# Weight and bias of a normalisation: one GpSimd operation over four chunks in place of one for each chunk

## The chip, the cores and the metric

The kernel runs on one core of a Trainium2 chip. The metric is device time in microseconds of one launch. The median of three runs is 2514.97 us (2506.65 to 2515.73). The engines are named as in the profile: PE is TensorE, DVE is VectorE, ACT is ScalarE, POOL is GpSimd, SP is SyncE, which here only issues DMAs.

## The reference

Four cross-attention layers run over `x` of 2 x 1024 tokens with 288 channels, with a context of 2 x 154 tokens. Layers 0 and 1 are blocks of three parts with quantised linear maps; layers 2 and 3 are plain attention over two parts of the context. A block of layers 0 and 1, cut to what matters:

```python
def quant_act(x):
    s = max(abs(x), axis=-1) / 127 + 1e-8
    q = clip(round(x / s), -127, 127)
    return q, s, sum(q, axis=-1)

def layer_norm(x, g, b, eps):
    return (x - mean(x)) * rsqrt(var(x) + eps) * g + b      # over the 288 channels

h = layer_norm(x, ln1_g, ln1_b, 1e-6);  q8, s, sm = quant_act(h)
q, k, v = (quant_linear(q8, s, sm, w, b) for w, b in (wq1.., wk1.., wv1..))
x = x + quant_linear(*quant_act(attn(q, k, v)), wo1, bo1)   # self-attention, 16 heads of 18
h = layer_norm(x, ln2_g, ln2_b, 1e-5)                       # then attention over the context
...
h = layer_norm(x, ln3_g, ln3_b, 1e-5)                       # then 288 -> 1152, gelu, 1152 -> 288
```

The weight `g` and the bias `b` of each normalisation are rows of 288 numbers, the same for every token.

## The kernel before

The tokens lie on the 128 partitions in 16 chunks of 128 tokens (`x` is `[128, 16, 288]`, float32, and stays in SBUF). Work on tokens is done in groups of four chunks (`HC = 4`, 512 tokens).

`ln_quantise` normalises and quantises one such group. VectorE computes mean and variance of each chunk (`bn_stats`, `bn_aggr`, L406 and L407) and adds epsilon (L408); GpSimd raises to the power -1/2 (L411); VectorE makes the shift (L413). Then, chunk by chunk, ScalarE writes `x * rstd + shift` into the tile `h` of `[128, 4, 288]` (L419), and engine `eng` multiplies by the weight and adds the bias, in place (L427): two operations of 128x288 for each of four chunks. `eng` is GpSimd, but for the first two calls, which `prepare_first` makes with VectorE. The weight and the bias are broadcast to all partitions beforehand, in a tile `ln` of `[128, 2, 288]` (`load_ln`, L175).

`quantise` follows: VectorE takes the largest magnitude of each chunk's rows in one reduction over the whole tile (L370), a scale (L371) and its reciprocal (L372); GpSimd writes the reciprocal into extra columns in three bfloat16 parts (L377 to L380); VectorE scales each chunk (L382), ScalarE rounds it and sums it (L386), VectorE writes the sums (L396, L397). Then TensorE transposes (L443), and the linear maps run.

`ln_quantise` runs 24 times: for the self-attention of each layer and batch (tile names `ah` for the two on VectorE, `alh` for six), for the attention over the context (`blh`, eight), and for the feed-forward part (`clh`, eight).

All this is side work. The main stream is attention: TensorE makes logits twice, once by query for their row maxima, which VectorE reduces (L597, L604), and once by key (L656), which ScalarE exponentiates (L658) and TensorE multiplies with the values (L670). GpSimd splits the maxima in three parts (L210 to L213), TensorE transposes them (L572), and ScalarE's and SP's DMAs bring them back as extra rows of the queries. GpSimd also splits queries and keys (L507, L514), adds results to `x` (L469), fills constant rows (L106), finishes weight preparation (L245 to L260; VectorE's share is L222 to L240), and issues the DMAs that load weights (L197, L1393).

What order the instructions have: the program interleaves the main stream with the side work by counts (`beside` and the generators' `yield`s), and the whole body stands in one block that a planner orders, `tc.block(schedule_with_timeline_sim=True)`: it places each instruction on its engine by a clock of its own. Each engine then runs its own list strictly in that order. The order on GpSimd in the trace isn't that of the program: other operations stand between the eight of a normalisation at several places.

Of the kernel before, what the change touches and what calls it, by code (L numbers as in the profile page):

```python
# [13 lines left out]
ALU = mybir.AluOpType  # L14
AX = mybir.AxisListType

P = 128
B, S, C, T = 2, 1024, 288, 154
# [3 lines left out]
HC = 4  # L22
# [31 lines left out]
def tile_xattn(ctx: ExitStack, tc: tile.TileContext, ins: dict, out: bass.AP):  # L54
# [81 lines left out]
    def big(name):  # L136
        return work.tile([P, FF], F32, tag="big", name=name, bufs=3)

    def bf(name):
        return work.tile([P, 3 * HQ], BF16, tag="bf", name=name, bufs=3)  # L140
# [11 lines left out]
    def view(ap, **kw):  # L152
        names = list(kw)
        return ap.rearrange(f"p ({' '.join(names)}) -> p {' '.join(names)}", **kw)
# [209 lines left out]
    def quantise(h, q, s, n, width, name):  # L364

        st = small.tile([P, 4, HC], F32, tag="qstat", name=name)
        am, rs, qs, r = (st[:, j, 0:n] for j in range(4))
        nc.vector.tensor_reduce(am, h, AX.X, ALU.max, apply_absolute_value=True)  # L370
        nc.vector.tensor_scalar(s, am, 1.0 / 127.0, 1e-8, ALU.mult, ALU.add)  # L371
        nc.vector.reciprocal(rs, s)  # L372

        def cols(k0, k1):
            return q[:, :, width + k0 : width + k1]

        nc.gpsimd.tensor_copy(cols(9, 12), rs.unsqueeze(2).to_broadcast([P, n, 3]))  # L377
        nc.gpsimd.tensor_tensor(r, rs, q[:, :, width + 9], ALU.subtract)
        nc.gpsimd.tensor_copy(cols(7, 9), r.unsqueeze(2).to_broadcast([P, n, 2]))
        nc.gpsimd.tensor_tensor(q[:, :, width + 6], r, q[:, :, width + 7], ALU.subtract)  # L380
        for c in range(n):
            nc.vector.tensor_scalar(  # L382
                h[:, c, :], h[:, c, :], rs[:, c : c + 1], MAGIC, ALU.mult, ALU.add
            )
        for c in range(n):
            nc.scalar.activation(  # L386
                q[:, c, 0:width],
                h[:, c, :],
                AF.Identity,
                bias=nmagic,  # L390
                scale=1.0,
                accum_out=qs[:, c : c + 1],
            )
        sums = qs.unsqueeze(2).to_broadcast([P, n, 3])
        hi = q[:, :, width : width + 6 : 2]
        nc.vector.tensor_scalar(hi, sums, -1.0, None, ALU.mult)  # L396
        nc.vector.scalar_tensor_tensor(  # L397
            q[:, :, width + 1 : width + 6 : 2], sums, -1.0, hi, ALU.mult, ALU.subtract
        )

    def ln_quantise(c0, ln, eps, s, name, h=None, q=None, eng=nc.gpsimd):
        st = small.tile([P, HC, 6], F32, tag="bn", name=f"{name}st")
        mv = small.tile([P, HC, 2], F32, tag="mv", name=f"{name}mv")
        rstd = small.tile([P, HC], F32, tag="rstd", name=f"{name}r")
        for c in range(HC):
            nc.vector.bn_stats(st[:, c, :], x[:, c0 + c, :])  # L406
            nc.vector.bn_aggr(mv[:, c, :], st[:, c, :])  # L407
        nc.vector.tensor_scalar(  # L408
            rstd, mv[:, :, 1:2].rearrange("p c a -> p (c a)"), eps, None, ALU.add
        )  # L410
        nc.gpsimd.tensor_tensor(rstd, rstd, neghalf, ALU.pow)  # L411
        shift = small.tile([P, HC], F32, tag="shift", name=f"{name}sh")
        nc.vector.scalar_tensor_tensor(  # L413
            shift.unsqueeze(2), mv[:, :, 0:1], -1.0, rstd.unsqueeze(2), ALU.mult, ALU.mult
        )
        if h is None:
            h = view(big(f"{name}h"), c=HC, w=C)
        for c in range(HC):
            nc.scalar.activation(  # L419
                h[:, c, :],  # L420
                x[:, c0 + c, :],
                AF.Identity,
                bias=shift[:, c : c + 1],
                scale=rstd[:, c : c + 1],
            )
            for j, op in ((0, ALU.mult), (1, ALU.add)):
                eng.tensor_tensor(h[:, c, :], h[:, c, :], ln[:, j, :], op)  # L427
        if q is None:
            q = bf(f"{name}q")
        q = view(q[:, 0 : HC * CZ], c=HC, w=CZ)  # L430
        quantise(h, q, s, HC, C, f"{name}qs")
        return q
# [517 lines left out]
    class SelfAttention:  # L950
# [26 lines left out]
        def prepare(self):  # L977
            w, b, name = self.w, self.b, self.name
            self.begin()
            for hf in range(2):  # L980
                c0 = b * 8 + hf * HC
                s = small.tile([P, HC], F32, tag="st", name=f"{name}st")
                q = ln_quantise(c0, w["ln"], 1e-6, s, f"{name}l")
                yield 8
                qT = transposed(q, f"{name}t")
                sb = token_scales(s, f"{name}sb")
                yield 2
                yield from weights_of(2, linear_T(qT, w["k"], sb, self.k[hf], f"{name}k"))
                self.values(hf, qT, s)
                yield 3  # L990
                yield from weights_of(2, linear_T(qT, w["q"], sb, self.q[hf], f"{name}q"))

        def prepare_first(self):
# [12 lines left out]
            def normalise(hf):  # L1006
                h = apool.tile([P, HC, C], F32, tag="a", name=f"{name}h", bufs=2)
                s = small.tile([P, HC], F32, tag="st", name=f"{name}st")
                c0 = b * 8 + hf * HC
                q = ln_quantise(  # L1010
                    c0, w["ln"], 1e-6, s, f"{name}l", h, tile(), nc.vector
                )
                scales.append(s)
                qs.append(q)
# [151 lines left out]
    def cross_attention(w, b, name):  # L1166
# [71 lines left out]
        def queries(hf):  # L1238
            s = small.tile([P, HC], F32, tag="st", name=f"{name}st")
            q = ln_quantise(b * 8 + hf * HC, w["ln"], 1e-5, s, f"{name}l")  # L1240
            yield 8
            qT = transposed(q, f"{name}t")
            sb = token_scales(s, f"{name}sb")
            rows.append(new_rows(f"{name}qr"))
            yield 2
            yield from weights_of(2, linear_T(qT, w["q"], sb, rows[hf], f"{name}q"))
# [491 lines left out]
```

## Time and profile before

| | us |
|---|---|
| median of three runs | 2514.97 |
| the profiled execution | 2516.42 |
| its span, first to last instruction | 2514.6 |
| PE busy | 1970.1 (78%) |
| DVE busy | 1865.4 (74%) |
| ACT busy | 1394.9 (55%) |
| POOL busy | 786.6 (31%) |
| L427 on POOL, 176 instructions of 128x288 | 135.1 (49.4 + 49.1 + 36.6) |
| L427 on DVE, 16 instructions of 128x288 | 6.2 |
| L419 on ACT, one chunk | 0.61 |
| mean granted TensorE clock | 0.867 |

A line of a group reads: source line, engine, operation, output<-inputs, shapes, count, busy us and mean ns of one, idle time of the engine before them and what ended it. A line of the timeline reads: start and length in us of neighbouring instructions of one kind taken together, engine, line, operation, tiles, count, and in brackets the idle time before and what ended it. The chain is the work that ended last, followed back step by step; its pieces read start, length, what.

### The profile page before, as it was taken

What the parts mean: (1) busy time and instruction counts of PE and PEld (TensorE: products, weight loads), DVE (VectorE), ACT (ScalarE), POOL (GpSimd) and SP (SyncE); (2) the same over time, 40 slices, a digit from 0 to 9 for tenths busy, and PEclk for the clock granted to TensorE, in tenths of its full rate; (3) what the DMA queues carried; (4) which work ended last, traced back from release to release, by engine and by line L of the source; (5) the groups of instructions that cost most, each with busy time, mean ns of one, the idle gap of its engine ahead of it and who ended that gap; (6) DMA issues with size and microseconds to landing.
All of it is one profiled execution on the core that took longest, in us unless ns stands there. A gap on an engine that the chain in (4) does not pass through costs nothing.

```text
span 2514.6 us, 33307 instructions
## 1 busy us (share of the span) xinstructions
PE 1970.1 (78%) x10524; PEld 851.0 (34%) x10524; DVE 1865.4 (74%) x4465; ACT 1394.9 (55%) x2639; POOL 786.6 (31%) x1794
## 2 busy tenths in 40 slices
PE   1679998888776878887678678887777887788987
PEld 1233333332333233323333233333334333443443
DVE  6789997899775659998569849994346786555665
ACT  3267766555576665556666355557654444654443
POOL 5424224211325451132353530223255132422210
PEclk9589998899787989999889689896888888888998
DMA  3423212211001322110032131100133210212221
GB/s 95 150 66 94 70 42 55 75 55 28 16 9 44 113 74 58 44 29 13 7 101 72 29 88 49 34 9 12 32 82 92 73 47 27 64 45 80 75 65 36
DMA packets 160129, 141.56 MB, mean 56 GB/s; under 512 B 44251, under 2 KB 156467, under 8 KB 159888
## 3 DMA queue, kind: packets, MB, share of 16 engines
q1 hardware_dynamic: 148528, 120.58, 16.6%
q0 software_dynamic: 3840, 13.37, 2.1%
q10 hardware_dynamic: 7584, 5.47, 1.2%
q8 instruction: 84, 1.38, 0.2%
q14 instruction: 93, 0.76, 0.1%
HBM read 96.60 MB, written 39.37 MB: 54 GB/s over the span
## 4 chain that ended last, share of the span: by engine, by line
PE 25%; DVE 15%; ACT 10%; DMA 6%; issue 3%; POOL 3%; SPq 1%; ACTq 0%; DVEq 0%; POOLq 0%
DVE L_xattn_amxh L604 4%; PE L_xattn_aato L670 4%; PE L_xattn_o L1484 3%; PE L_xattn_aats L656 3%; ACT L_xattn_aatse L658 3%; PE L_xattn_ato L670 2%; PE L_xattn_ats L656 2%; PE L_xattn_amx L597 2%; PE L_xattn_q L453 2%; DVE L_xattn_batse L742 2%; ACT L_xattn_atse L658 1%; DMA L_xattn_bqT<-L_xattn_bmxsr 1%; DVE L_xattn_bmxm L637 1%; DVE L_xattn_bmxn L642 1%; DVE L_xattn_mxn L642 1%
## 5 line engine op out<-in xcount | busy, mean ns | idle before, releaser
L658 ACT ACTIVATE L_xattn_aatse<-L_xattn_aats 128x512 f32<-128x512 f32 x1024 | 574.6, 595 | 300.5 <-PE L_xattn_aats L656 283.4
L604 DVE TENSOR_REDUCE L_xattn_amxh<-L_xattn_amx 128x1 f32<-128x512 f32 x1024 | 658.7, 677 | 54.6 <-PE L_xattn_amx L597 50.6
L656 PE MATMUL L_xattn_aats<-L_xattn_aqT,kT 120*128 120x512 bf16 x1024 | 392.9, 409 | 99.9 <-ACT L_xattn_aatse L658 61.6
L597 PE MATMUL L_xattn_amx<-kT,L_xattn_aqT 108*128 108x512 bf16 x1024 | 394.7, 418 | 64.2 <-DVE L_xattn_amxh L604 46.7
L670 PE MATMUL L_xattn_aato<-L_xattn_aatse,L_xattn_av 128*32 128x512 f32 x2048 | 296.9, 649 | 28.7 <-ACT L_xattn_aatse L658 26.3
L656 PEld LDWEIGHTS <-kT 120*128 120x128 bf16 x1024 | 96.2, 101 | 334.3 <-issue 297.6
L658 ACT ACTIVATE L_xattn_atse<-L_xattn_ats 86x512 f32<-86x512 f32 (+1 forms) x256 | 142.5, 589 | 109.6 <-PE L_xattn_ats L656 102.2
L597 PEld LDWEIGHTS <-L_xattn_aqT 108*128 108x128 bf16 x1024 | 103.4, 103 | 218.0 <-issue 164.9
L642 DVE TENSOR_REDUCE L_xattn_mxn<-L_xattn_mx 128x2 f32<-128x172 f32 (+1 forms) x512 | 125.1, 302 | 35.1 <-PE L_xattn_mx L627 34.6
L743 ACT ACTIVATE L_xattn_batse<-L_xattn_batse 128x512 f32<-128x512 f32 x160 | 100.0, 626 | 85.6 <-DVE L_xattn_batse L742 82.5
L656 PE MATMUL L_xattn_ats<-L_xattn_qT,L_xattn_kT 120*86 120x512 bf16 (+1 forms) x256 | 101.5, 432 | 40.6 <-DMA L_xattn_qT<-L_xattn_mxsr 20.0
L742 DVE TENSOR_TENSOR L_xattn_batse<-L_xattn_bats,L_xattn_bmT 128x512 f32<-128x512 f32 x160 | 107.3, 680 | 23.9 <-PE L_xattn_bats L670 12.2
L637 DVE TENSOR_TENSOR L_xattn_bmxm<-L_xattn_bmx,L_xattn_bm 128x308 f32<-128x308 f32 x256 | 114.8, 464 | 5.5 <-PE L_xattn_bmx L627 4.6
L642 DVE TENSOR_REDUCE L_xattn_bmxn<-L_xattn_bmxm 128x2 f32<-128x308 f32 x256 | 113.8, 457 | 0.3
L1484 PE MATMUL L_xattn_o<-wo,L_xattn_p 128*128 128x288 f32 x320 | 100.8, 452 | 6.2 <-DVE L_xattn_p L815 4.7
L670 PEld LDWEIGHTS L_xattn_aato<-L_xattn_aatse,L_xattn_av 128*32 128x32 f32 x2048 | 42.0, 111 | 162.1 <-ACT L_xattn_aatse L658 131.9
L627 PE MATMUL L_xattn_bmx<-L_xattn_bkT,L_xattn_bqT 108*128 108x154 bf16 x512 | 76.5, 248 | 16.7 <-DVE L_xattn_amxh L604 8.2
L627 PE MATMUL L_xattn_mx<-L_xattn_kT,L_xattn_qT 108*128 108x154 bf16 x512 | 72.0, 257 | 22.1 <-DVE L_xattn_mxn L642 7.6
L843 DVE STREAM_TRANSPOSE L_xattn_atT<-L_xattn_ato 128x512 f32<-128x512 f32 x64 | 45.7, 713 | 57.4 <-PE L_xattn_ato L670 47.0
L1351 PE MATMUL L_xattn_co<-L_xattn_wfc2t,L_xattn_cgT 117*128 117x288 bf16 x320 | 63.6, 350 | 22.4 <-ACT L_xattn_cgT L1348 21.5
L670 PE MATMUL L_xattn_ato<-L_xattn_atse,L_xattn_v 68*32 68x512 f32 (+1 forms) x512 | 74.1, 651 | 5.2 <-ACT L_xattn_atse L658 4.7
L1484 PEld LDWEIGHTS L_xattn_o<-wo,L_xattn_p 128*128 128x128 f32 x320 | 64.0, 210 | 30.7 <-DVE L_xattn_p L815 6.0
(629 smaller groups left out, 3729.2 us busy)
## 6 DMA issues: line engine op xcount, KB each, us to landing
kT<-L_xattn_akr SPq DMA_DIRECT2D x192, 72.0 KB
L_xattn_aqT<-L_xattn_aqr SPq DMA_DIRECT2D x192, 72.0 KB
L_xattn_bqT<-L_xattn_bqr SPq DMA_DIRECT2D x192, 72.0 KB
L_xattn_qT<-L_xattn_r SPq DMA_DIRECT2D x192, 72.0 KB
L_xattn_akr<-L_xattn_akst SPq DMA_DIRECT2D x16, 324.0 KB
L_xattn_aqr<-L_xattn_aqst SPq DMA_DIRECT2D x16, 324.0 KB
L_xattn_bqr<-L_xattn_bqst SPq DMA_DIRECT2D x16, 324.0 KB
L_xattn_r<-L_xattn_qst SPq DMA_DIRECT2D x16, 324.0 KB
```

The costliest lines, as they stand in the source:

```text
L597: nc.tensor.matmul(sp, lhsT=qt[:KR, j, c * P : (c + 1) * P], rhs=kt[:KR, j, a * 512 : (a + 1) * 512], start=True, stop=True,)
L604: nc.vector.tensor_reduce(halves[:, a, c, j, :], sp, AX.X, ALU.max, negate=True)
L627: nc.tensor.matmul(sp[:, j * T : (j + 1) * T], lhsT=qt[:KR, 2 * a + j, c * P : (c + 1) * P], rhs=kt[:KR, 4 * g + 2 * a + j, 0:T], start=Tr ...
L637: nc.vector.tensor_tensor(lm, of, mask[:, c : c + 1, 0:T].to_broadcast([P, 2, T]), ALU.add)
L642: nc.vector.tensor_reduce(nm[:, c, 2 * a : 2 * a + 2, n], of[:, :, k0:k1], AX.X, ALU.max, negate=True,)
L656: nc.tensor.matmul(sp, lhsT=keys(j), rhs=qt[:KM, j, :], start=True, stop=True)
L658: nc.scalar.activation(e, sp, AF.Exp)
L670: made = nc.tensor.matmul(po[32 * i : 32 * i + 32, :], lhsT=lhsT, rhs=rhs, start=start, stop=stop)
L742: nc.vector.tensor_tensor(e, sp, maskT[:, m, :], ALU.add)
L743: nc.scalar.activation(e, e, AF.Exp)
L1351: nc.tensor.matmul(ps, lhsT=gT[:, k, :], rhs=qw2[:, k, :], start=(k == 0), stop=(k == 9),)
L1484: nc.tensor.matmul(ps, lhsT=t[:, c * P : (c + 1) * P], rhs=wo[:, u0 + u, :], start=(u == 0), stop=(u == len(tiles) - 1),)
```

## The change

The two operations leave the loop over the chunks. They run once each, over all four chunks, with the weight's and the bias's row read four times over:

```diff
@@ ln_quantise @@
         for c in range(HC):
             nc.scalar.activation(h[:, c, :], x[:, c0 + c, :], ...)
-            for j, op in ((0, ALU.mult), (1, ALU.add)):
-                eng.tensor_tensor(h[:, c, :], h[:, c, :], ln[:, j, :], op)
+        for j, op in ((0, ALU.mult), (1, ALU.add)):
+            eng.tensor_tensor(
+                h, h, ln[:, j : j + 1, :].to_broadcast([P, HC, C]), op
+            )
         if q is None:
             q = bf(f"{name}q")
```

Each element has the same arithmetic in the same order. Of 192 operations of 128x288, 176 on GpSimd and 16 on VectorE, 48 of 128x1152 are left, 44 and 4. The multiplication now reads what all four ScalarE instructions have written. Nothing else of the program's text differs; lines below it move by two.

## The prediction

> **What bounds the kernel now.** I read the page first, then the groups of GpSimd by shape, the line of the change (L427) with its waits, the timeline at each of its places, and the chain.
>
> ```profile
> PE 1970.1 (78%) x10524; PEld 851.0 (34%) x10524; DVE 1865.4 (74%) x4465; ACT 1394.9 (55%) x2639; POOL 786.6 (31%) x1794
> PE 25%; DVE 15%; ACT 10%; DMA 6%; issue 3%; POOL 3%; SPq 1%; ACTq 0%; DVEq 0%; POOLq 0%
> ```
>
> TensorE and VectorE set the time; GpSimd is busy for 31% and has 3% (some 75 us) of the chain that ended last. So what GpSimd saves counts only where it stands on that chain, or where another engine waits for it.
>
> ```profile
> L427 POOL TENSOR_TENSOR L_xattn_blh<-L_xattn_blh,L_xattn_ln 128x288 f32<-128x288 f32 x64 | 49.4, 798 | 9.9 <-ACT L_xattn_blh L419 9.6
> L427 POOL TENSOR_TENSOR L_xattn_clh<-L_xattn_clh,L_xattn_ln 128x288 f32<-128x288 f32 x64 | 49.1, 795 | 14.9 <-ACT L_xattn_clh L419 14.8
> L427 POOL TENSOR_TENSOR L_xattn_alh<-L_xattn_alh,L_xattn_ln 128x288 f32<-128x288 f32 x48 | 36.6, 798 | 6.0 <-ACT L_xattn_alh L419 6.0
> L507 POOL TENSOR_TENSOR L_xattn_bqy<-L_xattn_bqy,L_xattn_bqst 108x512 f32<-108x512 f32 x24 | 27.8, 1164 | 42.8 <-ACT L_xattn_bqst L506 37.4 <-DMA L_xattn_bqT<-L_xattn_bqr 5.4
> L212 POOL TENSOR_TENSOR L_xattn_amxn<-L_xattn_amxn,L_xattn_amxst 128x16 f32<-128x16 f32 x32 | 7.2, 224 | 1.8
> ```
>
> The changed work is 64 + 64 + 48 = 176 GpSimd instructions, 22 normalisations of eight, plus 16 on VectorE in the first two. Who waits for them, from the view of that line:
>
> ```profile
> its engine sat idle before it (us, times) until:
>   ACT L_xattn_clh L419: 14.8, 4
> ...
> who waited for it (us, times):
>   PEld L443: 0.9, 1
> ```
>
> Nobody, to speak of. VectorE's reduction L370, the first reader of the normalised chunks, never stands idle for GpSimd. One ordinary place in the timeline shows why:
>
> ```profile
> 386.59 2.17 ACT L419 ACTIVATE L_xattn_blh<-x,L_xattn_blsh,L_xattn_blr 128x288 f32<-128x288 f32 x4
> 387.28 6.08 POOL L427 TENSOR_TENSOR L_xattn_blh<-L_xattn_blh,L_xattn_ln 128x288 f32<-128x288 f32 x8 [2.40 <-ACT L_xattn_blh L419]
> 388.23 3.08 DVE L604 TENSOR_REDUCE L_xattn_amxh<-L_xattn_amx 128x1 f32<-128x512 f32 x5 [0.36 <-PE L_xattn_amx L597]
> 395.94 1.34 DVE L370 TENSOR_REDUCE L_xattn_blqs<-L_xattn_blh 128x4 f32<-128x1152 f32 x1
> ```
>
> ScalarE writes the four chunks back to back, GpSimd follows 0.69 us after the first, ends at 393.36, and L370 starts 2.58 us later from VectorE's own queue. Over all 22 places this margin is 1.1 to 44 us, mostly 2.6 to 6.4.
>
> **The change, step by step.**
>
> *One instruction of 128x1152.* No row shows it. Fixed part from the 16-element row: about 200 ns; the rest of 796 ns by four: 200 + 4 x 596 = 2.58 us. Low end: the 108x512 row adds 368 ns for 224 elements, so 796 + 864 x 1.64 = 2.21 us. High end: no fixed cost saved, 4 x 0.796 = 3.18 us. I take 2.58: same engine, partitions and type.
>
> *GpSimd time.* Eight back to back start 0.76 us apart (6.08 / 8); two take some 5.1 us (range 4.4 to 6.3). Saving 22 x 1.0 = 22 us of its queue, nearly all beside TensorE and VectorE. On the chain the timeline of pieces has 24 of the 176, 17.6 us together, at three places only (1714, 1828, 2145); the largest pieces:
>
> ```profile
> 1713.82 3.81 POOL L_xattn_clh L427 x5
> 2145.53 4.50 POOL L_xattn_clh L427 x6
> ```
>
> Times 1.0/6.08 this is **-2.9 us**.
>
> *A wait added.* The first instruction now needs ScalarE's fourth chunk: the series starts 2.2 us after the first ACTIVATE, not 0.69. In 11 of the 22 places GpSimd starts later than that first chunk anyway (behind its own queue, or with the last chunk); there nothing or little is lost. In the other 11 it loses 1.5 us and wins 1.0 back: +0.5, against margins of 1.1 and more in front of L370, so nothing; without that cover 11 x 0.5 = 5.5 us. Behind the waiting instruction stand GpSimd's small splits of the maxima (L210 to L213) and the third parts (L514), whose readers are TensorE's transposes and SP's transfers. On the chain the wait costs: at 1714 1.45 us (start 1713.82, last chunk 1715.28), at 1828 0.9, at 2145 0.4: **+2.7 us**.
>
> *The start of the kernel*, on VectorE:
>
> ```profile
> 35.01 2.18 ACT L419 ACTIVATE L_xattn_ah<-x,L_xattn_alsh,L_xattn_alr 128x288 f32<-128x288 f32 x4 [13.99 <-DVE L_xattn_alsh L413]
> 35.97 3.03 DVE L427 TENSOR_TENSOR L_xattn_ah<-L_xattn_ah,L_xattn_ln 128x288 f32<-128x288 f32 x8
> 36.14 3.64 POOL L245 TENSOR_SCALAR L_xattn_wq1sq<-L_xattn_wq1w 108x864 bf16<-108x864 f32 x1 [2.75 <-DVE L_xattn_wq1w L240]
> ```
>
> VectorE's rows (444 ns at 288, 0.68 us at 512 in L507) give 1.05 ns an element: 444 + 864 x 1.05 = 1.35 us, two 2.65. They begin at 37.2 and end near 39.9, not at 38.99: +0.9. On the other side L245, 0.90 us just before this, took 3.64 beside the eight; with VectorE waiting until 37.2 it could finish, and the queue behind it leads to TensorE's first transposes at 49.00: down to -2.7. I take **0**, between them: later in that queue L377 waits for VectorE's row maximum anyway.
>
> *Longer holds of a shared port.* Today:
>
> ```profile
> 1269.48 1.93 DVE L228 SCALAR_TENSOR_TENSOR L_xattn_wfc_0s<-L_xattn_wfc_0s 96x3 f32<-96x3 f32 x1
> ...
> 1269.49 1.16 POOL L507 TENSOR_TENSOR L_xattn_aky<-L_xattn_aky,L_xattn_akst 108x512 f32<-108x512 f32 x1
> 1270.61 0.79 POOL L427 TENSOR_TENSOR L_xattn_alh<-L_xattn_alh,L_xattn_ln 128x288 f32<-128x288 f32 x1
> ```
>
> A VectorE instruction with two SBUF inputs, 0.15 us elsewhere, stood 1.93 us, until two GpSimd instructions had ended; L604, which reads PSUM, isn't touched (five in 3.08 us at 388.23). Summing over the trace each VectorE duration above the tenth percentile of its line and shape (those over 0.15 us), 52 us are lost so, 23 of them beside L427, and 9.9 of the 52 (19%) lie on the chain. Here a rule speaks against the change: the Trainium skill, "SBUF — State Buffer", in the table of terms and the summary of ports, says that the pair shared by VectorE and GpSimd is held for the full instruction and that the loser fully blocks. By the row alone (so much wait per us of GpSimd work) 23 us shrink with the work, 23 x 5.1/6.08: -3.7 us, -0.7 on the chain, and the whole sum would come to -0.9. By the rule the wait grows with the instruction: 8.4 of the 23 us are four waits that already spanned several instructions and stay; the other 14.5 us are some 24 waits of 0.6 us, which become half an instruction, 1.29 us, at 5.1/6.08 as many occasions: 26 us, so +11.5, of which 19% counts: **+2.2 us**. I take the rule, since the row shows such a wait ending with the GpSimd instruction.
>
> *Order.* The order on each engine comes from a planner that runs its own clock, so new durations can swap neighbours anywhere. No row prices that: one 0.6 us instruction on the wrong side at each of 22 places, all of one sign, is 13 us either way. I take 0 and keep 13 for the range.
>
> Sum: -2.9 + 2.7 + 0 + 2.2 = **+2.0 us** on this execution's 2516.42 us (span 2514.6, 1.8 around it). The execution lies 1.5 us above the median of the runs, 2514.97; on that the forecast is **2517 us**.
>
> **Rivals.**
>
> *Slower: the port decides.* The place is weight preparation (L224 to L240), the quantisations (L382, L396, L397) and the context's keys (L510), with L604 queued behind and TensorE waiting for L604. For it: from 126 to 504 us VectorE is busy 331 of 378 us, so waits there have no slack. If each of the 24 waits lasts a whole instruction less what it is now, half the way (1.0 us more each, 24 us), and 74% (VectorE's busy share) counts, it is +18: 2533 us. From 17 us of added waits at that share it passes 0.5% (12.6 us), about what a measurement of this kernel can tell from no change. Against it: only 19% counts in the chain today.
>
> *Faster: the shorter series is passed on.* In the 11 places where the series began late it would end 0.9 us sooner; -9.9 if L370 moves up with it, -2.7 at the start, -2.9 on the chain: about 2500 us. Against it: L370's margins.
>
> *The two cost what eight did.* If reading the same row four times breaks the instruction up, 3.18 us each: 6.36, +0.8 on the chain's 17.6 us in place of -2.9, +2.7 for the wait, +2.2 or a little more for the port: 2521 us, still no change.
>
> *The new order alone* moves either of these by its 13 us.
>
> **How the numbers follow.** Nearly even 0.46, port 0.28, passed on 0.21, no cheaper 0.05. Likeliest: 2517, its own range 2504 to 2530 (the order's 13 us). For 8 in 10 both other cases are reached with part of their spread: 2496 to 2541. Beyond 0.5% means under 2502.4 or over 2527.5: faster 0.25 (most of "passed on", an edge of the first), slower 0.30, same 0.45.
>
> **What would show it.** The changed line with 44 GpSimd instructions at 2.2 to 2.7 us and 4 at 1.35 on VectorE; GpSimd's busy time near 760 us; the series starting with ScalarE's last chunk; L370 still not waiting for GpSimd. Right on the port: VectorE durations of L228, L382 or L510 reaching 2 us beside L427, and VectorE's busy time up by about 10 us. Wrong if L370 waits for L427, if the splits L210 move late and TensorE waits for their transposes, or if groups far from L427 change their idle time by more than 10 us: then the order decided.

## The result and the profile after

The changed kernel took 2526.29 us (median of its runs, 2519.58 to 2531.66), beside 2511.3 us for the kernel before on the same chip: ratio **1.0048, 95% interval 1.0032 to 1.0064**. Run again later beside the experiments, it gave 1.0038 (1.0022 to 1.0053). So it is slower by 0.4 to 0.5%, by these ratios some 10 to 12 us, at the edge of what the prediction called no change (the two medians of the first set differ by 15.0 us, those of the second, 2522.61 and 2514.64, by 8.0). The profiled execution took 2526.29 us, its span 2524.5.

The page of the changed kernel: busy times, and the chain by engine. From the changed line down to the end of the file all line numbers are two higher than before (L604 is now L606).

```profile
PE 1972.2 (78%) x10524; PEld 846.8 (34%) x10524; DVE 1870.1 (74%) x4453; ACT 1395.9 (55%) x2639; POOL 763.5 (30%) x1662
PE 39%; DVE 26%; ACT 16%; DMA 10%; issue 4%; POOL 3%; SPq 1%; ACTq 0%; DVEq 0%; POOLq 0%
```

GpSimd does 23 us less work, VectorE 5 us more. The shares of the chain can't be set against those of before: here they add up to 99%, there to 63%, because the chain of the kernel before is followed back only to 921.8 us and that of the changed kernel to its start. In us, GpSimd has 68.3 on the one and 68.8 on the other. Nothing in these two lines accounts for 10 us. The groups of GpSimd by shape, and the view of the changed line:

```profile
L427 POOL TENSOR_TENSOR L_xattn_blh<-L_xattn_blh,L_xattn_ln 128x1152 f32<-128x1152 f32 x16 | 42.2, 2641 | 18.3 <-ACT L_xattn_blh L419 18.0
L427 POOL TENSOR_TENSOR L_xattn_clh<-L_xattn_clh,L_xattn_ln 128x1152 f32<-128x1152 f32 x16 | 41.9, 2621 | 8.2 <-ACT L_xattn_clh L419 8.0
L427 POOL TENSOR_TENSOR L_xattn_alh<-L_xattn_alh,L_xattn_ln 128x1152 f32<-128x1152 f32 x12 | 31.8, 2656 | 11.8 <-ACT L_xattn_alh L419 11.6
L509 POOL TENSOR_TENSOR L_xattn_bqy<-L_xattn_bqy,L_xattn_bqst 108x512 f32<-108x512 f32 x24 | 27.6, 1156 | 40.1 <-ACT L_xattn_bqst L508 37.5 <-DMA L_xattn_bqT<-L_xattn_bqr 2.5
```

```profile
who waited for it (us, times):
  POOL L_xattn_ln L175: 0.3, 1
```

One of these instructions takes 2.6 us (estimated: 2.58), and VectorE still never stands idle for it. The place at 387 us in the timeline after: ScalarE's four chunks, GpSimd's series starting 0.08 us after the fourth, 5.34 us long in place of 6.08. It ends at 393.88, and L370 starts at 396.42 from its own queue, 2.54 us later (2.58 before).

```profile
386.29 2.17 ACT L419 ACTIVATE L_xattn_blh<-x,L_xattn_blsh,L_xattn_blr 128x288 f32<-128x288 f32 x4
388.54 5.34 POOL L427 TENSOR_TENSOR L_xattn_blh<-L_xattn_blh,L_xattn_ln 128x1152 f32<-128x1152 f32 x2 [4.46 <-ACT L_xattn_blh L419]
396.42 1.34 DVE L370 TENSOR_REDUCE L_xattn_blqs<-L_xattn_blh 128x4 f32<-128x1152 f32 x1
```

The start of the kernel, on VectorE, with the freed GpSimd instruction L245 (3.64 us before, 0.91 now):

```profile
34.20 2.18 ACT L419 ACTIVATE L_xattn_ah<-x,L_xattn_alsh,L_xattn_alr 128x288 f32<-128x288 f32 x4 [11.99 <-DVE L_xattn_alsh L413]
35.33 0.91 POOL L245 TENSOR_SCALAR L_xattn_wq1sq<-L_xattn_wq1w 108x864 bf16<-108x864 f32 x1 [2.75 <-DVE L_xattn_wq1w L240]
36.41 2.75 DVE L427 TENSOR_TENSOR L_xattn_ah<-L_xattn_ah,L_xattn_ln 128x1152 f32<-128x1152 f32 x2 [1.17 <-ACT L_xattn_ah L419]
```

**Where the time went.** I matched the main stream's reductions and exponentials one by one between the two traces and took the difference of their starts, as a median over stretches of 25 us; I call it the drift. Up to 600 us the changed kernel is level or a little ahead (-1.4 us). Between 600 and 850 us it falls back by 10.2 us, between 1175 and 1250 us by another 6.8; elsewhere it wavers by a few us and by the end some of it has been given back. The two places have the same nature. There the side work of a stretch (feed-forward of one half, preparation of the next layer) drains while the reductions of the main stream stand still; I call such a standstill a stop. The last reduction before the first of the two, and the first one after it, in VectorE's timeline of the kernel before and of the changed one, each with the first of the side work's reciprocals near it (L372):

```profile
719.21 0.19 DVE L372 RECIPROCAL L_xattn_cqs<-L_xattn_cs 128x1 f32<-128x1 f32 x2
...
728.95 1.29 DVE L604 TENSOR_REDUCE L_xattn_amxh<-L_xattn_amx 128x1 f32<-128x512 f32 x2 [0.79 <-PE L_xattn_amx L597]
...
822.69 0.69 DVE L604 TENSOR_REDUCE L_xattn_amxh<-L_xattn_amx 128x1 f32<-128x512 f32 x1 [1.08 <-PE L_xattn_amx L597]
```

```profile
726.89 0.69 DVE L606 TENSOR_REDUCE L_xattn_amxh<-L_xattn_amx 128x1 f32<-128x512 f32 x1 [0.16 <-PE L_xattn_amx L599]
727.50 0.21 DVE L372 RECIPROCAL L_xattn_cqs<-L_xattn_cs 128x1 f32<-128x1 f32 x2
...
831.58 0.69 DVE L606 TENSOR_REDUCE L_xattn_amxh<-L_xattn_amx 128x1 f32<-128x512 f32 x1 [1.44 <-PE L_xattn_amx L599]
```

The stop grew from 93.1 us (from the start of the last reduction, the second of the two, at 729.6, to the next start, 822.7) to 104.7. The second stop went from 96.7 to 106.2 us. Ahead of the first, the main stream is earlier than in the kernel before (by 2.7 us at its last reduction, by up to 9.9 a little sooner) and the side work later (its reciprocals by 8.3). Ahead of the second, the main stream gains up to 7.7 us on the drift of 7.4 that it has there. That can be the order of things, or a delay in the side work. Which one, the experiments had to tell.

### The profile page after: what moved, and what is told of

It is laid out like the page before. It is cut to its first block, busy times and chain, and to the rows that moved or that the text cites. A ratio compares the mean times of both kernels' runs of the same rounds, so it can differ in the third digit from the quotient of the medians.

```text
span 2524.5 us, 33183 instructions
## 1 busy us (share of the span) xinstructions
PE 1972.2 (78%) x10524; PEld 846.8 (34%) x10524; DVE 1870.1 (74%) x4453; ACT 1395.9 (55%) x2639; POOL 763.5 (30%) x1662
## 4 chain that ended last, share of the span: by engine, by line
PE 39%; DVE 26%; ACT 16%; DMA 10%; issue 4%; POOL 3%; SPq 1%; ACTq 0%; DVEq 0%; POOLq 0%
DVE L_xattn_amxh L606 9%; PE L_xattn_aato L672 7%; PE L_xattn_aats L658 5%; ACT L_xattn_aatse L660 5%; PE L_xattn_amx L599 4%; PE L_xattn_o L1486 3%; PE L_xattn_q L455 2%; DVE L_xattn_batse L744 2%; PE L_xattn_ato L672 2%; PE L_xattn_ats L658 2%; DMA L_xattn_bqT<-L_xattn_bmxsr 2%; DMA L_xattn_aqT<-L_xattn_amxsr 2%; ACT L_xattn_atse L660 2%; DVE L_xattn_bmxm L639 2%; DVE L_xattn_bmxn L644 1%
## 5 line engine op out<-in xcount | busy, mean ns | idle before, releaser
L606 DVE TENSOR_REDUCE L_xattn_amxh<-L_xattn_amx 128x1 f32<-128x512 f32 x1024 | 661.0, 682 | 62.0 <-PE L_xattn_amx L599 59.4
L599 PEld LDWEIGHTS <-L_xattn_aqT 108*128 108x128 bf16 x1024 | 102.6, 103 | 216.5 <-issue 162.6
L745 ACT ACTIVATE L_xattn_batse<-L_xattn_batse 128x512 f32<-128x512 f32 x160 | 100.1, 626 | 96.2 <-DVE L_xattn_batse L744 90.4
L672 PEld LDWEIGHTS L_xattn_aato<-L_xattn_aatse,L_xattn_av 128*32 128x32 f32 x2048 | 41.8, 111 | 175.3 <-ACT L_xattn_aatse L660 150.3
L1353 PE MATMUL L_xattn_co<-L_xattn_wfc2t,L_xattn_cgT 117*128 117x288 bf16 x320 | 67.7, 366 | 25.5 <-ACT L_xattn_cgT L1350 24.4
L629 PEld LDWEIGHTS <-L_xattn_bqT 108*128 108x128 bf16 x512 | 45.7, 104 | 82.8 <-issue 51.5
```

What stands on the lines that cost most here:

```text
L599: nc.tensor.matmul(sp, lhsT=qt[:KR, j, c * P : (c + 1) * P], rhs=kt[:KR, j, a * 512 : (a + 1) * 512], start=True, stop=True,)
L606: nc.vector.tensor_reduce(halves[:, a, c, j, :], sp, AX.X, ALU.max, negate=True)
L629: nc.tensor.matmul(sp[:, j * T : (j + 1) * T], lhsT=qt[:KR, 2 * a + j, c * P : (c + 1) * P], rhs=kt[:KR, 4 * g + 2 * a + j, 0:T], start=Tr ...
L672: made = nc.tensor.matmul(po[32 * i : 32 * i + 32, :], lhsT=lhsT, rhs=rhs, start=start, stop=stop)
L745: nc.scalar.activation(e, e, AF.Exp)
L1353: nc.tensor.matmul(ps, lhsT=gT[:, k, :], rhs=qw2[:, k, :], start=(k == 0), stop=(k == 9),)
```

## The experiments

The theories. **Order:** the planner, whose clock sees other GpSimd instructions, interleaves the streams differently, and puts main-stream work ahead of side work shortly before a drain. **Port:** GpSimd's 2.6 us holds stop VectorE's instructions of the side work. **Wait:** GpSimd's new wait for ScalarE's fourth chunk delays what follows.

To separate them I held the order. At the end of the kernel function every instruction is chained to the one that is to stand ahead of it on its engine, from a packed list; these chains carry order only, no waits:

```diff
+    for lane, packed in ORDER.items():
...
+        for k in picks:
+            i = left.pop(k)
+            if before is not None:
+                tc.add_manual_dep(i, before.name, no_wait, reason="order")
+            before = i
```

ORDER is the order of all five engines in the kernel before ("old") or in the changed kernel ("new"), with the weight-and-bias instructions of a normalisation in the places of those that they replace (as the traces show it, two in the fourth and the last of the eight places; four, as a rule, in the second or third, the fourth, the seventh and the last; eight, or four, all at the first of two). In the traces of the kernels that hold one list all other instructions of GpSimd, VectorE and SP stand exactly as in the kernel that it comes from, and those of TensorE and ScalarE do but for a few records.

**The two long ones in the old order** (the changed kernel with that list).

> The two long operations, with every other instruction of every engine held to the order that it has in the kernel before (chains of order without waits). If the new order of the planner makes the loss, this is not slower than before: ratio to it 0.997 to 1.002 (my sum of the prediction without its term for order gave +2.0 us; with the measured waits at the shared port, +3). If the longer holds of the port make it by themselves, most of the +12 us stays: ratio 1.003 to 1.006. If the wait for ScalarE's fourth chunk makes it, the same, and the third experiment shows it too.

Measured 1.0017 (0.9998 to 1.0037). VectorE's first stop pair here lies at 727.26 and 820.10 us:

```profile
727.26 1.29 DVE L619 TENSOR_REDUCE L_xattn_amxh<-L_xattn_amx 128x1 f32<-128x512 f32 x2 [0.79 <-PE L_xattn_amx L612]
...
820.10 0.69 DVE L619 TENSOR_REDUCE L_xattn_amxh<-L_xattn_amx 128x1 f32<-128x512 f32 x1 [1.21 <-PE L_xattn_amx L612]
```

The stop is 92.2 us, as before the change, and the drift has no jump. The change itself, without its order, costs a few us at most: +1.9 ± 2.4 when the runs are put to an equal clock, as the table below has it. (The interval of the ratio alone still reaches into the range that was to speak for the port.)

**The eight short ones in the new order** (the kernel before with the other list).

> The eight short operations of the kernel before, put where the changed kernel has its two, and every other instruction of every engine held to the order of the changed kernel. If the order makes the loss, it is as slow as the changed kernel or a little slower (the eight take 6.1 us and not 5.3): ratio to before 1.003 to 1.007. If the long holds of the port make it, ratio 0.998 to 1.002.

Measured 1.0022 (1.0007 to 1.0037): slower, though every instruction is that of the kernel before. It lies between its two expectations, so the order by itself makes a part of the loss, by these ratios about half. The stops are 104.1 and 102.3 us. VectorE's timeline just before the first stop, in the kernel before:

```profile
717.14 1.87 DVE L604 TENSOR_REDUCE L_xattn_amxh<-L_xattn_amx 128x1 f32<-128x512 f32 x3
718.92 0.20 DVE L371 TENSOR_SCALAR L_xattn_cs<-L_xattn_cqs 128x1 f32<-128x1 f32 x2
...
719.21 0.19 DVE L372 RECIPROCAL L_xattn_cqs<-L_xattn_cs 128x1 f32<-128x1 f32 x2
...
719.39 0.81 DVE L382 TENSOR_SCALAR L_xattn_ch<-L_xattn_ch,L_xattn_cqs 128x1152 f32<-128x1152 f32 x1
721.00 0.69 DVE L604 TENSOR_REDUCE L_xattn_amxh<-L_xattn_amx 128x1 f32<-128x512 f32 x1 [0.80 <-PE L_xattn_amx L597]
721.60 0.81 DVE L382 TENSOR_SCALAR L_xattn_ch<-L_xattn_ch,L_xattn_cqs 128x1152 f32<-128x1152 f32 x1
```

and in this kernel, where the list shifts all lines by 13 (L617 is L604, L385 is L372, L395 is L382):

```profile
723.18 1.86 DVE L617 TENSOR_REDUCE L_xattn_amxh<-L_xattn_amx 128x1 f32<-128x512 f32 x3
724.96 0.20 DVE L384 TENSOR_SCALAR L_xattn_cs<-L_xattn_cqs 128x1 f32<-128x1 f32 x2
...
728.49 1.29 DVE L617 TENSOR_REDUCE L_xattn_amxh<-L_xattn_amx 128x1 f32<-128x512 f32 x2 [3.16 <-PE L_xattn_amx L610]
729.69 0.21 DVE L385 RECIPROCAL L_xattn_cqs<-L_xattn_cs 128x1 f32<-128x1 f32 x2
...
729.96 1.54 DVE L395 TENSOR_SCALAR L_xattn_ch<-L_xattn_ch,L_xattn_cqs 128x1152 f32<-128x1152 f32 x2
```

The side work's maxima (L371) are ready, but two reductions of the main stream stand ahead of its reciprocals, and wait 3.16 us for TensorE. The reciprocals come 10.5 us later than before, in an execution that was 3.2 us behind at 600 us, while main-stream reductions run up to 7 us ahead. The main stream then has nothing to do until the side work is through: what it gained is idle time, and at this place what the side work lost is paid in full (reciprocals 7.3 us late beyond the 3.2, drift +7.5). Over the whole kernel it isn't: the two jumps of this kernel make 13.4 us, its loss is 5.5 ± 2.1 us at equal clock.

**Eight short ones, after the fourth chunk.** The order came out as in the kernel before, without any list.

```diff
-            for j, op in ((0, ALU.mult), (1, ALU.add)):
-                eng.tensor_tensor(h[:, c, :], h[:, c, :], ln[:, j, :], op)
+        for c in (3, 0, 1, 2):
+            for j, op in ((0, ALU.mult), (1, ALU.add)):
+                eng.tensor_tensor(h[:, c, :], h[:, c, :], ln[:, j, :], op)
```

> Eight short operations in the order of before, but after ScalarE's four chunks, the fourth chunk first, so that GpSimd waits for ScalarE's last chunk as in the changed kernel; lengths and the order of all else are as before. If the added wait makes the loss: ratio 1.003 to 1.006. By my sum (2.7 us at three normalisations) 1.001; by the other theories 0.999 to 1.002.

Measured 0.9991 (0.9972 to 1.0011). In the old order the added wait costs nothing that could be measured; there the wait theory falls, and so does most of the +2.7 us that I had put down for it. It also shows that the planner changed its order for the number or the length of the instructions, not for this wait.

**Pairs, planned freely.**

```diff
+            if c % 2 == 0:
+                continue
             for j, op in ((0, ALU.mult), (1, ALU.add)):
-                eng.tensor_tensor(h[:, c, :], h[:, c, :], ln[:, j, :], op)
+                eng.tensor_tensor(
+                    h[:, c - 1 : c + 1, :],
+                    h[:, c - 1 : c + 1, :],
+                    ln[:, j : j + 1, :].to_broadcast([P, 2, C]),
+                    op,
+                )
```

> Four operations of 128x576, each for two chunks, planned freely (the planner finds a third order, unlike both). If longer holds of the port make the loss, they are half as long here and the loss is about half: ratio 1.001 to 1.004, and waits of VectorE beside these operations reach some 1.3 us. If the planner's order makes it, the time is a new draw, anywhere from 0.995 to 1.006, without regard to the length of the hold.

Measured 1.0007 (0.9992 to 1.0022): half the length of the hold, and no loss that could be measured. The planner's order is a third one, with stops of 99.3 and 107.2 us, but the main stream arrives at them 4 and 11 us sooner, and its standstill of 46 us at 405 us is gone (none of over 40 us there). VectorE's waits add up to as much as in the changed kernel (26.8 us, table below). It fits the order theory and does not by itself refute the other.

**The changed kernel again, and its order in parts.** The second stretch of side work, up to the first stop, was given one order and all the rest the other; across the seams the instructions of the later stretch stand slightly later.

> The changed kernel once more, beside the three that take it apart, on the same chip: ratio 1.003 to 1.006 as before.

> The two long operations, with the order of the kernel before, except for what belongs to the second side stretch (roughly 410 to 800 us, up to the point where the main stream waits for the side work to drain), which stands in the new order. If the drift of the traces is right (the changed kernel loses some 11 us between 690 and 800 us, by side work ordered later), this has most of the loss: 5 to 9 us more than the long operations in the old order alone, ratio to before 1.003 to 1.005, and the drift against before jumps at 700 to 800 us. If the loss is spread over the whole order, or is the new order's work at 1200 us, ratio 1.000 to 1.002.

> The counterpart: the changed kernel in its new order, except for the second side stretch, which stands in the old order. If the second stretch makes most of the loss: ratio 1.000 to 1.002, and no jump of the drift at 700 to 800 us. If it is the third stretch (1200 us) or spread: 1.003 to 1.005.

Measured 1.0038 (1.0022 to 1.0053), 1.0025 (1.0010 to 1.0041) and 1.0022 (1.0006 to 1.0038). The new order in the second stretch alone brings the first stop to 101.1 us and leaves the second at 97.4; the old order there alone brings 93.6 and 106.0. Each stop follows the order of its own stretch. In time, the expectation that the second stretch makes most of the loss failed: against the two long ones in the old order (1.0017, beside its own runs of before) it adds 0.0008, the rest of the order 0.0005, with intervals of 0.0015 to 0.002 either way on each of these ratios. The stops are told apart, their shares of the loss are not.

**Pairs in the new order.**

> Four operations of 128x576 in the order of the changed kernel: a hold of 1.4 us in place of 0.7 and 2.6. With the eight short in this order +5.5 us to before and the two long +11 to +13: if the rest is due to the length of the hold at the shared port, this lies between them, +7 to +9 us, ratio 1.0025 to 1.004, and the waits at the places where the long ones blocked VectorE for 2 us and more (some 707, 798, 891 and 1284 us) are 1.4 us or less. If it is due to the wait for the fourth chunk alone, it is as fast as the eight in this order, 1.0015 to 1.0025.

Measured 1.0025 (1.0010 to 1.0041), between the eight (1.0022) and the two (1.0038 and 1.0048) and near the eight. That is the border of its two expectations, so it doesn't tell the hold from the wait for the fourth chunk; the eight short ones after the fourth chunk, in the new order, weren't run. The place where the long ones stopped VectorE most clearly is L397 in the changed kernel, a 3-element operation between two SBUF inputs, held until 0.02 us past the end of GpSimd's instruction:

```profile
706.27 2.61 POOL L427 TENSOR_TENSOR L_xattn_clh<-L_xattn_clh,L_xattn_ln 128x1152 f32<-128x1152 f32 x1 [0.98 <-ACT L_xattn_clh L419]
706.62 2.28 DVE L397 SCALAR_TENSOR_TENSOR L_xattn_cg<-L_xattn_cqs,L_xattn_cg 128x3 bf16<-128x3 f32 x1
```

With pairs in the same order it takes what it takes elsewhere (L410 is L397 there):

```profile
706.78 0.16 DVE L410 SCALAR_TENSOR_TENSOR L_xattn_cg<-L_xattn_cqs,L_xattn_cg 128x3 bf16<-128x3 f32 x1
```

**Pairs in the old order.**

> Four operations of 128x576 in the order of the kernel before. Pairs lie between the eight short ones (1.000) and the two long ones in this order (1.0017 measured): ratio 0.999 to 1.002 if neither the length of the hold nor the wait matters much while the order stays; 1.002 or more only if the hold at the port costs by itself.

Measured 0.9982 (0.9966 to 0.9998), median 2503.26 us beside 2507.91, a little under what was expected. This is the one version that is faster than the kernel before, by some 4 us; its interval almost touches 1, and it is one of a dozen comparisons.

**Side work fed sooner.** If side work that is late at a drain costs, giving it out sooner should pay.

```diff
-            beside(main, 128, side, n, 112)
+            beside(main, 128, side, n, 104)
```

> The kernel before (eight short operations), planned freely, with the side work of the first three stretches given out by step 104 of the main stream's 128 and not by step 112. If the loss of the changed kernel is side work that is late when its stretch drains (the main stream's reductions stand still for 93 us from 730 us and for 97 us from 1201 us), side work that comes sooner shortens both stops: ratio 0.990 to 0.998. If the drains are set by the side work's own chain and not by when it is begun, or the planner puts the main stream first all the same: 0.998 to 1.004.

With 96 in place of 104:

> As the one before, by step 96. If side work late at the drains is what costs, more of the same: 0.985 to 0.997, unless the main stream is then starved within the stretch, 1.000 to 1.010.

With 104, in the changed kernel:

> The changed kernel (two long operations) with the side work given out by step 104. If the long operations' own cost is the +2 us that they have in the old order, this is within 0.3% of the eight short ones with the same feeding (the planner's order is another one again, which alone moved the time by up to 0.3%).

All three missed: 1.0164 (1.0127 to 1.0201), 1.0134 (1.0111 to 1.0157) and, with the long ones, 1.0092 (1.0069 to 1.0116). The stops at the drains did shorten (to 80 us each in the first), but the main stream now stands still in other places too: stops of over 40 us add up to 453 us in place of 315 (four of 46.0, 93.1, 96.7 and 79.2 before). So the remedy that the order theory suggests is not to be had from this number. Nor are the long ones within 0.3% of the short ones here; they are 0.7% faster (four runs each; at equal clock +15.3 ± 3.0 against +28.5 ± 3.6 us). Their orders differ and weren't held, so I draw nothing from that but the size of what an order can do.

All kernels with the feeding unchanged. Drift: how far the main stream falls back against the kernel before over each stretch. Stops: length of the two stops. Waits: VectorE's time above the tenth percentile of the same line and shape (those over 0.15 us), beside the weight-and-bias instructions on GpSimd. At equal clock: difference of the means in us with its 95% interval, corrected as told in the last section.

| GpSimd's instructions | order | drift 600 to 850 | drift 1175 to 1250 | stops | waits | ratio | at equal clock |
|---|---|---|---|---|---|---|---|
| 8 (before) | old | | | 93.1, 96.7 | 21.7 | 1 | |
| 8, after the fourth chunk | old | +0.4 | +0.2 | 92.6, 95.8 | 18.6 | 0.9991 | -1.7 ± 2.7 |
| 4 | old | -0.6 | +0.3 | 91.4, 95.0 | 18.5 | 0.9982 | -3.9 ± 2.9 |
| 2 | old | -0.8 | +0.1 | 92.2, 97.7 | 21.0 | 1.0017 | +1.9 ± 2.4 |
| 8 | new | +7.5 | +5.9 | 104.1, 102.3 | 10.8 | 1.0022 | +5.5 ± 2.1 |
| 4 | new | +7.3 | +5.8 | 104.2, 102.6 | 16.0 | 1.0025 | +5.7 ± 2.1 |
| 2 (after, twice) | new | +10.2, +9.6 | +6.8, +6.6 | 104.7, 106.2; 104.4, 106.1 | 25.7; 28.1 | 1.0048; 1.0038 | second: +7.9 ± 2.2 |
| 2 | new in 2nd stretch | +8.9 | +1.6 | 101.1, 97.4 | 25.2 | 1.0025 | +4.2 ± 2.3 |
| 2 | old in 2nd stretch | +2.0 | +6.6 | 93.6, 106.0 | 21.4 | 1.0022 | +6.1 ± 1.7 |
| 4 | a third, planned freely | +3.2 | +4.2 | 99.3, 107.2 | 26.8 | 1.0007 | -2.2 ± 1.8 |

No kernel in the old order falls back at these places, and every one in the new order does, whatever the length of its instructions. The jumps don't add up to the loss: 17 us in the changed kernel, against 10 to 12 us. Its second profiled execution falls back by 9.6 and 6.6 us and yet took 2516.46 us, as long as that of before (2516.42): it was 6.7 us ahead at 600 us and won back 6 us after 1300. And the pairs planned freely fall back at both places, have the second largest sum of waits, and lose nothing. So the stops show where an order acts; the time of the whole isn't read from them. Past 1300 us the drift falls again in nearly all traces, also in those in the old order (-2 to -5 for the two long ones), so a part of this belongs to the profiled execution of before; how much the new order gives back there is left open.

## Why the prediction was right, and where it was not

The time lay in the range (2496 to 2541), 9 us above the forecast of 2517, and on the slower side of no change. Against its own kernel before it is some 10 to 12 us where the sum gave +2.0; that this is inside the range is owed to the 13 us kept for an order of unknown sign, and in part to luck, as the sum's terms show. Point by point:

- **The new instructions.** Estimated 2.58 us each and 5.1 for two; measured 2.62 to 2.66 and 5.34. On VectorE 2.65 estimated, 2.75 measured. GpSimd is busy for 763.5 us where I had 760. With the pairs (1.40 us) the three sizes lie on one line, 0.19 us plus 2.1 ns an element; the fixed part that I had read from the 16-element row was about 0.2.
- **L370 not waiting for GpSimd, and the series starting with ScalarE's fourth chunk:** both as said. The rival in which the shorter series is passed on falls: its 9.9 us needed L370 to move up.
- **The start: 0.** The first two series end 0.2 us later and 0.4 us sooner than before (39.16 and 44.87, against 38.99 and 45.24). It was right.
- **The added wait: +2.7 us.** Too much. Eight short ones with this wait came out at -1.7 ± 2.7 us at equal clock.
- **The port: +2.2 us, from waits that grow by 11.5 and count for 19%.** Both factors were off. *The waits:* in the old order they didn't grow (21.7 to 21.0 us by the count of the table): they are longer, but 12 in place of 25. There the row alone, so much wait per us of GpSimd work, was nearer than the rule. In the new order they grew with the hold, 10.8, 16.0 and 25.7 to 28.1 us for holds of 0.8, 1.4 and 2.6 us, with none, none and 11 of over 1.5 us. So the rule of the Trainium skill ("SBUF — State Buffer", section "Terms", that the loser fully blocks) gives the length of a wait (2.28 us at 707), and the order decides how many there are. VectorE's busy time rose by 4.7 us, not by 10. *The weight:* the chain that gave 19% is followed back only to 921.8 us. Of the 52 us of waits 25.5 come after that, so its 9.9 us are 39% of what it could show. In the changed kernel's whole chain it is 35.2 of 55.5 us (63%), L397 at 707 among them:

```profile
706.71 2.19 DVE L_xattn_cg L397
```

"Only 19% counts" was therefore no argument against the rival in which the port decides (+18 us, 74% counted). It falls by the runs: with the old order the long ones cost +1.9 ± 2.4 us in all, and in the new order, from eight to two, the waits grow by 15 to 17 us and the time by 2.4 ± 3.0 at equal clock, where 74% would be 11 and more.
- **The sum of these: +2.0 us.** Held alone, by the old order, it measured +1.9 ± 2.4. That is better than its terms deserve: the wait and the growth of the port's waits were too large, the port's weight was misread, and the saving on the chain that stood against them (-2.9) was not measured by itself. All three were weighed by a chain that leaves out the first 922 us, with 80 of the 176 instructions and the first of the two stops.
- **The order: 0, with 13 us for the range.** This is the term that was mis-sized. It measured +5.5 ± 2.1 us with the instructions unchanged. With the +1.9 of the long ones in the old order that makes 7.4 us, and the changed kernel lost 7.9 ± 2.2 in its second measurement at equal clock. Whether something is left beyond that in the first, of 12 us, can't be told: it may be spread, or the two meeting, long holds that fall beside the side work where the new order has put it (the first drift is 9.6 to 10.2 with the two, 7.5 and 7.3 with eight and four). My sign that the order decided, groups far from L427 whose idle time changes by more than 10 us, showed: on TensorE's second attention product (28.7 us before, and on its weight loads, 162.1 to 175.3), on ScalarE's L743 (85.6 to 96.2) and on six groups of GpSimd, while the reductions stayed below it (54.6). With the old order it showed on one group for the two long ones, on two for the pairs, and on none for the eight after the fourth chunk. The two lines after the change:

```profile
L606 DVE TENSOR_REDUCE L_xattn_amxh<-L_xattn_amx 128x1 f32<-128x512 f32 x1024 | 661.0, 682 | 62.0 <-PE L_xattn_amx L599 59.4
L672 PE MATMUL L_xattn_aato<-L_xattn_aatse,L_xattn_av 128*32 128x512 f32 x2048 | 293.2, 644 | 39.3 <-ACT L_xattn_aatse L660 36.9
```

The other sign, TensorE waiting longer for the splits of the maxima (L213), didn't show: 49.1 us before, 49.9 after.

The sign of the order's effect couldn't be read from the profile of before; its place perhaps could. I spread the order over the 22 places of the change, one neighbour each, but that profile already had two stops of over 90 us in the main stream, and both jumps lie there. That other places take up such delays in their margins is argued, not shown.

## What to carry to other kernels

Where a planner sets the order, an edit to an engine with slack is first of all another order: to know what the edit itself does, hold the order of the old program and run the new instructions in it, then the old instructions in the new order. Look for what a new order does first where one stream stands still and waits for another: both jumps here lay at such places, though an order can win back elsewhere what it loses there. Before the share of a chain is used as a weight, add the shares up: here they came to 63%, and the chain had nothing to say of the first 922 us. Fewer and longer instructions on an engine that blocks another make fewer and longer waits; whether their sum grows depends on what the order puts beside them, so a middle size is worth a try (here the pairs, -3.9 ± 2.9 us in the old order).

## What the runs showed of the hardware

- **The granted clock goes with half of the spread.** Executions of one kernel differed by some 30 us (before: 2498.09 to 2529.0 us), and the granted clock with them, 0.858 to 0.876. A straight line fitted within the kernels gives 12.5 us less for each 0.01 of granted clock; with it the standard deviation within a kernel falls from 5.9 to 4.1 us, half of the variance. The last column of the table uses this line. It is a fit, not a cause shown: what makes the clock differ from one execution to the next wasn't tried.
- **VectorE's 3-element instruction is held for as long as one of 1152 elements on GpSimd.** L397 needs 0.16 us, took 2.28 us beside one, and a 96x3 instruction (L224) took 4.05 us across three GpSimd instructions in a row, at 1283.56 us of the changed kernel.
- **Broadcasting costs nothing more on GpSimd.** The same row read two or four times over in one instruction (1.40 and 2.62 us) lies on the line through two rows that aren't broadcast, 16 elements (0.224 us) and 288 (0.80 us).
